# Token records in seven-word list entries, and filter rows of 2048 bytes

## The chip, the cores and the metric

The kernel runs on one core of a Trainium2 chip. Its engines are named as the profile names them: PE multiplies matrices (PEld is its weight load), DVE does elementwise work, ACT applies functions with a scale and a bias per row, POOL issues the indirect DMAs (gathers and scatters by lists of indices), SP issues all other DMAs. On chip there are SBUF, where every tile has 128 partitions, and PSUM, which PE writes.

The metric is the device time of one execution in microseconds (us). Before the change the median of six runs is 1482.05 us, with 1470.3 and 1488.45 as the ends.

## The reference, cut to what matters

The input is 16,384 tokens (16 x 1024) of 512 float32 values.

```python
xn = _layernorm(x)
# attention part
D = _fractal_dimension(xn)                       # one number, from the first 1024 values
x1 = ifft(fft(xn) * _wave_filter(D, 512)).real
lat = x1 @ W_el + b_el                           # 24 latents per token
bits = (sigmoid(lat) > 0.5)
s = x1 + _golay_correct(bits) @ W_le + b_le
# mixture of experts, 8 experts, the best 2 for each token
probs = softmax(xn @ router_w.T)
topk_vals, topk_idx = top_k(probs, 2)
topk_w = topk_vals / (topk_vals.sum(-1) + 1e-06)
combined = xn @ expert_weights[topk_idx]         # two products of 512 x 512 per token
g = _silu(((combined + topk_vals) * topk_w).sum())
out = x + s * g
```

`_golay_correct` takes 12 parity sums over the 24 bits and, if one to three of them are set, flips bits among the first 12.

## The kernel before

**Pass 1** goes through the tokens in order, in 128 tiles of 128 tokens, four tiles to a block. The filter is a circulant real operator, so it is worked out as matmuls in a basis in which a row's sum half, difference half and remaining half stay apart. For tile `g`:

- DVE adds the two halves of the row (`total`, L446); ACT turns the row's sum into a mean (`level`, L459) and takes the squares' sum (`spread`, L465); from it comes the token's scale (`scale`, L483 to L494).
- DVE folds the row (`fold`, L504 to L509), PE transposes it (`transpose`, L516) and ACT copies it out (L518).
- PE multiplies (`filt`): the sum part with `cs` (L532, 128 filter columns and 32 columns for latents and router logits), the difference part with `cd` (L533, the same widths), the rest with `cm` (L535). ACT scales the result into the block's buffer `yb` (L538), and every four tiles SP stores it into `yd` in DRAM (`store`, L545), a row of 576 words to a token: 128 columns of the sum, 32 + 32 latent columns, 128 of the difference, 256 of the rest.
- The latents and logits (`take_ex`, L561) go to `code` every 8 tiles: bits by comparison (L571), transposed through PE and ACT, parity sums by PE (L590), `correct` on DVE (L597 to L607). ACT copies the 12 bits that never change into the token's record (L588), `correct` writes the other 12 into it.
- They also go to `route` in eight rounds of 16 tiles: some 45 DVE operations and a few matmuls choose the two experts, the weights and the place of each token in one of 28 lists, one for each pair of experts. A record has 32 words a token: two weights, the bias (word 9), mean and scale (10, 11), the token's number (12), bits as bf16 (from word 13). At the end of a round 16 scatters on POOL (`scatter`, L787; one for each tile of 128 tokens) write words 10 to 12 of each record into `lists`, and `put_records` (L624) writes the whole records into the 32 columns `Q:XQ` of `yd`, four DMAs on SP a round.

101 tiles are filled by tokens of one pair of experts alone ("whole" tiles). Their entries are read by `whole_ops`, in two parts of 30 and 71 tiles: one gather `tt` (L907), taken apart by word on DVE (L918, L921), transposed on PE (L928), kept (L931 to L935). The other tiles fetch their entries one by one.

**Pass 2** takes tiles in the order of the lists: 28 whole tiles (the lead), 61 "item" tiles (leftovers of a pair, one expert at a time, results stored to `ed`), 5 whole tiles, and 27 "rest" tiles (which gather two stored item results) among 68 whole ones. For each tile POOL gathers the entry (`entry`, `rentry`), the token's `x` row (`xg`) and its filter row (`yg`, L1072 through `gather`; 8 buffers), and scatters the finished row (`put`, L1387). DVE normalises (L1237), ACT splits into halves (L1253), SP's transposing DMA turns them (L1258), ACT joins them (L1262), PE multiplies (L1295, 16 matmuls to a whole tile). ACT scales the first product with the weight from the record in `yg` (`scaled`, L1342), DVE adds the second with the other weight, and ACT applies silu with the bias (`added`, L1350, L1353). For the filter part DVE copies the bits three times (`triple`, L1310), PE turns them (`turn_code`, L1316) and multiplies them with `wle3`, three bf16 terms of `W_le` (`mend`, L1328). `spread_out` adds that to the row in two steps (L1333, L1334) and undoes the halves (L1336 to L1339); `combine` forms the result (L1381, L1382). "Item" tiles do none of these filter steps.

The order on every engine is that in which the code issues its instructions. Pass 1 runs a fixed list of steps per tile, with one scatter, one step of `code` and four of `route` among them. Pass 2 has due times per tile (`triple` three tiles ahead, `turn_code` two, `mend` one), and 3 scatters of the last round per tile until they are gone. `cs`, `cd` and `cm` are scaled and laid out once, in a setup that ends ahead of the first tile; `wle3` is filled from `setup_code`, two steps a tile. `clear` fills the four record buffers with zeros and a constant 1 for the `b_le` row.

## Time and profile before

| | |
|---|---|
| time of the profiled execution | 1480.49 us |
| its span, first to last instruction | 1478.7 us |
| mean granted clock of PE | 0.940 |
| PE busy | 1292.4 us (87%) |
| DVE busy | 913.2 us (62%) |
| ACT busy | 848.5 us (57%) |
| POOL busy | 768.7 us (52%) |
| L1295, the experts' products | 2104 matmuls, 605 ns each, 952.6 us |
| L535, L532, L533, the filter's products | 159.3, 66.6 and 61.1 us |
| L787, scatters | 128, 1031 ns each, 132.0 us |
| L1072 into `yg` | 101, 1118 ns each, 112.9 us |
| `yd<-yb` | 32 DMAs of 1152 KB |
| `yd<-rec` | 32 DMAs of 64 KB |
| packets under 512 bytes | 199543 of 265017 |

A profile is one execution. Busy is the time in which an engine has an instruction at work; the time ahead of an instruction in which its engine has nothing to do is put down to the one that released it, or to "issue" where the profile shows nothing that was waited for, or to "remote" where the releaser is not found among the recorded ones. The windows view gives the busy time of every engine in a stretch of time. Pass 1 ends at about 395 us. A group's count can lie a little under the true one, since some records are missing.

### The profile page before, as it was taken

The page shows a single profiled execution, that of the slowest core. Times are in us where ns is not written, and L with a number is a line of the kernel's source. Part 1 is how long each engine was busy: PE and PEld are TensorE (multiplying, and loading weights), DVE is VectorE, ACT ScalarE, POOL GpSimd, SP SyncE. Part 2 cuts the span into 40 slices and gives each one's busy share as a digit, 9 for nine tenths or more (in the row PEclk, how much of TensorE's full clock was granted, in tenths as well). Part 3 has the DMA queues.
Part 4 walks back from the last instruction along what each step waited for, and adds up shares of the span by engine and source line. Part 5 has one row for each costly group of instructions (what it writes and reads, how often), then busy time and mean ns, then how long its engine had stood idle before and what let it go on. Part 6 is the DMA issues. An engine that isn't in the chain of part 4 may idle for free.

```text
span 1478.7 us, 17021 instructions
## 1 busy us (share of the span) xinstructions
PE 1292.4 (87%) x4128; PEld 689.2 (47%) x4128; DVE 913.2 (62%) x2837; ACT 848.5 (57%) x1439; POOL 768.7 (52%) x743
## 2 busy tenths in 40 slices
PE   6977866977969699992989989998999999999996
PEld 5856755765624244440334434443444444444442
DVE  7866855865557368960111112787778777787885
ACT  7966855765434245551667676555555555555553
POOL 0044134224365755566656521677777776776741
PEclk9988878988989899996899999999999999999999
DMA  7996545743634476473879995788888888887861
GB/s 243 396 281 190 190 150 161 236 166 110 199 97 103 108 184 142 116 175 96 191 181 220 206 234 149 200 209 206 210 202 223 208 211 212 214 220 192 216 180 50
DMA packets 265017, 276.45 MB, mean 187 GB/s; under 512 B 199543, under 2 KB 200439, under 8 KB 260826
## 3 DMA queue, kind: packets, MB, share of 16 engines
q1 hardware_dynamic: 217114, 139.62, 37.0%
q0 software_dynamic: 47264, 135.54, 31.7%
q8 instruction: 37, 0.61, 0.2%
q14 instruction: 58, 0.48, 0.1%
q10 hardware_dynamic: 544, 0.21, 0.1%
HBM read 144.81 MB, written 89.59 MB: 159 GB/s over the span
## 4 chain that ended last, share of the span: by engine, by line
PE 62%; issue 10%; ACT 8%; another core or an unknown queue 7%; DVE 7%; DMA 2%; POOL 1%; ACTq 1%; SPq 0%; POOLq 0%; DVEq 0%
PE pe L1295 44%; PE py L535 7%; PE pt L516 3%; PE py L532 2%; ACT no L465 2%; PE py L533 2%; DVE acc L1350 1%; ACT yb L538 1%; DMA plt<-pl 1%; ACT pmt L518 1%; ACT xt L1262 1%; ACTq L1342 1%; PE pg L1328 1%; POOL out L1387 1%
## 5 line engine op out<-in xcount | busy, mean ns | idle before, releaser
L1295 PE MATMUL pe<-w_sb,xt 128*128 x2104 | 952.6, 605 | 54.7 <-ACT xt L1262 34.0
L1295 PEld LDWEIGHTS pe<-w_sb,xt 128*128 128x128 f32 x2104 | 404.1, 194 | 520.6 <-issue 465.2
L787 POOL DMA_INDIRECT lists<-rec,dst x128 | 132.0, 1031 | 284.7 <-ACT pmt L518 146.3
L1353 ACT ACTIVATE acc<-acc,yg 128x512 f32<-128x512 f32 x129 | 92.6, 719 | 252.6 <-DVE acc L1350 178.0
L1262 ACT COPY xt<-plt 128x1024 uint16<-128x1024 uint16 x156 | 209.0, 1340 | 22.3 <-DMA plt<-pl 21.2
L1350 DVE SCALAR_TENSOR_TENSOR acc<-pe,yg,acc 128x512 f32<-128x512 f32 (+1 forms) x102 | 75.7, 743 | 177.2 <-PE pe L1295 87.5
L1253 ACT COPY pl<-xn 128x1024 uint16<-128x1024 uint16 x156 | 162.1, 1039 | 0.0
L1237 DVE TENSOR_SCALAR xn<-xg,mean,entry 128x512 f32<-128x512 f32 x61 | 36.3, 595 | 200.8 <-ACT pl L1253 169.2
L1072 POOL DMA_INDIRECT yg<-yd,toks x101 | 112.9, 1118 | 90.4 <-ACT acc L1353 37.9
L535 PE MATMUL py<-cm,pmt 128*128 128x288 f32 x512 | 159.3, 437 | 0.0
L538 ACT ACTIVATE yb<-py,rec 128x640 f32<-128x640 f32 x128 | 102.2, 798 | 93.2 <-remote 42.2
L1387 POOL DMA_INDIRECT out<-xg,toks x100 | 108.9, 1089 | 70.9 <-DVE xg L1382 44.6
L1342 ACT ACTIVATE acc<-pe,yg 128x512 f32<-128x512 f32 x101 | 68.6, 680 | 132.4 <-PE pc L1316 32.7
L532 PE MATMUL py<-cs,pmt 128*128 128x160 f32 x256 | 66.6, 345 | 74.1 <-ACT pmt L518 47.6
L1072 POOL DMA_INDIRECT xg<-in_x,toks x100 | 106.7, 1067 | 46.4 <-issue 29.1
L535 PEld LDWEIGHTS py<-cm,pmt 128*128 128x128 f32 x512 | 99.7, 209 | 16.3
L465 ACT ACTIVATE no<-xt,sum 128x512 bf16<-128x512 f32 x128 | 91.8, 717 | 0.9 <-DVE pp L446 0.9
L1072 POOL DMA_INDIRECT part<-ed,adr_r x54 | 60.6, 1122 | 60.3 <-DMA ed<-res 44.2
L1382 DVE TENSOR_TENSOR xg<-mix,xg 128x512 f32<-128x512 f32 (+1 forms) x128 | 88.0, 687 | 4.4
L1072 POOL DMA_INDIRECT entry<-lists,adr_i x61 | 62.6, 1026 | 53.9 <-DVE mean L1236 28.9
L1381 DVE TENSOR_TENSOR mix<-mix,acc 128x512 f32<-128x512 f32 x129 | 87.7, 680 | 0.2 <-ACT acc L1353 0.2
L518 ACT COPY pmt<-pt 128x512 f32<-128x512 f32 x128 | 73.9, 578 | 18.5 <-remote 16.5
(282 smaller groups left out, 1627.8 us busy)
## 6 DMA issues: line engine op xcount, KB each, us to landing
yd<-yb SPq DMA_DIRECT2D x32, 1152.0 KB
xt<-in_x SPq DMA_DIRECT2D x32, 1024.0 KB
ed<-res SPq DMA_DIRECT2D x61, 256.0 KB
w_sb<-in_expert_w SPq DMA_DIRECT2D x8, 1024.0 KB
plt<-pl SPq DMA_TRANSPOSE x156
lists<-rec,dst POOLq DMA_INDIRECT x128
yd<-rec SPq DMA_DIRECT2D x32, 64.0 KB
yg<-yd,toks POOLq DMA_INDIRECT x101
```

What stands on the lines that cost most here:

```text
L465: nc.scalar.activation(no, xts[g // TPT][:, g % TPT, :], AF.Square, bias=k.sum[:, j : j + 1], scale=-float(E), accum_out=k.sq2[:, j : j + 1],)
L532: nc.tensor.matmul(py[:, 0, 0:XQ], pmt[:, 0, :], cs, start=True, stop=False)
L535: nc.tensor.matmul(py[:, 1, 0 : X + H], pmt[:, 2 + c, :], cm[:, c, :], start=(c == 0), stop=(c == 1))
L538: nc.scalar.activation(y_room(g), py[:, :, 0:WY], AF.Copy, scale=k.rec[:, j, 11:12])
L787: dma = nc.gpsimd.indirect_dma_start(out=lists, out_offset=bass.IndirectOffsetOnAxis(ap=st.dst[:, j : j + 1], axis=0), in_=st.rec.bitcast( ...
L1072: nc.gpsimd.indirect_dma_start(out=dst, out_offset=None, in_=src, in_offset=bass.IndirectOffsetOnAxis(ap=idx, axis=0), bounds_check=limit - 1,
L1253: nc.scalar.copy(k.pl.rearrange("p (h e) -> p h e", h=2), k.xn.bitcast(U16).rearrange("p (e h) -> p h e", h=2),)
L1262: nc.scalar.copy(k.xt.bitcast(U16).rearrange("p c (t h) -> p h c t", h=2), k.plt.rearrange("p (h c) t -> p h c t", h=2),)
L1295: nc.tensor.matmul(pe.unsqueeze(1), k.xt[:, c, :], w_sb[:, bass.ds(e, 1), c, :], start=(c == 0), stop=(c == KC - 1),)
L1350: nc.vector.scalar_tensor_tensor(k.acc[:, c], src[:, c], k.rec[:, 1:2], k.acc[:, c], ALU.mult, ALU.add)
L1353: nc.scalar.activation(k.acc[:, c], k.acc[:, c], AF.Silu, bias=k.rec[:, 9:10])
L1387: dma = nc.gpsimd.indirect_dma_start(out=of, out_offset=bass.IndirectOffsetOnAxis(ap=k.tok, axis=0), in_=k.x, in_offset=None, bounds_check ...
```

## The change

A list entry now has seven words and holds the whole record: two weights, bias, mean, scale, token and the 24 corrected bits as one whole number. Entries have 28 bytes rather than 12. The 32 record columns leave `yd`, whose rows become 512 words (2048 bytes) rather than 576 (2304).

- `put_records` and `clear` are gone, and ACT's copy of 12 bits (L588). `correct` writes the corrected bits in place, multiplies all 24 with powers of two and sums them into the word `BITS`: two more DVE operations, 16 times.
- The scatter sends words 0 to 6.
- `filt` writes the sum's and the difference's results by turns of 32 columns into PSUM (`by_turns`), with the latents and logits in the first 64 columns. `cs` has its latent columns in front. The stored 512 columns come behind the latents. `wle3` is filled in the same order: six copies rather than three.
- `whole_ops` takes seven words apart, with seven transposes rather than three and four DVE operations in `kept` rather than three.
- Weights, bias and bits come from the entry, not from the `yg` record.
- `triple` is a bitwise and of the tile's bits word with the powers of two (128 x 32 int32) and a comparison (128 x 96, to bf16) rather than one copy. For the entries past 24, whose power is 0, the comparison gives the constant 1 that the `b_le` row needs.
- `spread_out` adds the whole PSUM row in one operation (128 x 512) rather than in two of half the size; its last four operations stay, two of them reading and writing by turns of 32.

```diff
@@ -20,9 +20,8 @@
-META = 32
-ENTRY = slice(10, 13)
-BITS = 26
+W0, W1, BIAS, MEAN, SCALE, TOKEN, BITS, META = range(8)
+ENTRY = META
...
@@ -101,8 +99,8 @@
-    lists = dram.tile([NPAIR * N, 3], I32, name="lists")
-    yd = dram.tile([N, ROW], F32, name="yd")
+    lists = dram.tile([NPAIR * N, ENTRY], I32, name="lists")
+    yd = dram.tile([N, E], F32, name="yd")
...
@@ -249,10 +249,6 @@
-    def clear(r):
-        nc.vector.memset(r, 0.0)
-        nc.vector.memset(bits_of(r)[:, :, L : L + 1], 1.0)
-
...
@@ -375,10 +369,19 @@
+
+        def kept(k):
+            r = slice(32 * k, 32 * k + 32)
+            v.tensor_copy(
+                by_turns(wle3[r, 0:H]), term[r, 0:H].rearrange("p (a q c) -> p a q c", a=2, c=C)
+            )
+            v.tensor_copy(wle3[r, H:E], term[r, H:E])
+
...
+            lambda: v.tensor_copy(bit_i, bit_r),
@@ -391,15 +394,13 @@
-            lambda: v.tensor_copy(wle3[0:32, :], term[0:32, :]),
+            lambda: kept(0),
...
-                lambda k=k: v.tensor_copy(
-                    wle3[32 * k : 32 * k + 32, :], term[32 * k : 32 * k + 32, :]
-                ),
+                lambda k=k: kept(k),
...
@@ -517,6 +515,9 @@
+    def by_turns(a):
+        return a.rearrange("p (q a c) -> p a q c", a=2, c=C)
+
     def y_room(g: int):
@@ -529,14 +530,18 @@
-        nc.tensor.matmul(py[:, 0, 0:XQ], pmt[:, 0, :], cs, start=True, stop=False)
-        nc.tensor.matmul(py[:, 0, XQ:WY], pmt[:, 1, :], cd, start=False, stop=True)
+        both = by_turns(py[:, 0, 0:WY])
+        for a, w in enumerate((cs, cd)):
+            nc.tensor.matmul(
+                both[:, a], pmt[:, a, :], w.rearrange("p (q c) -> p q c", c=C),
+                start=(a == 0), stop=(a == 1),
+            )
         for c in range(2):
...
         nc.scalar.activation(
-            y_room(g), py[:, :, 0:WY], AF.Copy, scale=k.rec[:, j, 11:12]
+            y_room(g), py[:, :, 0:WY], AF.Copy, scale=k.rec[:, j, SCALE : SCALE + 1]
         )
@@ -544,7 +549,7 @@
             out=yd[b * BLK : (b + 1) * BLK, :].rearrange("(p j) n -> p j n", p=P),
-            in_=ybs[b].rearrange("p j h n -> p j (h n)")[:, :, 0:ROW],
+            in_=ybs[b].rearrange("p j h n -> p j (h n)")[:, :, 2 * X : 2 * X + E],
         )
@@ -558,7 +563,7 @@
         y = ybs[b][:, first:past]
-        nc.vector.tensor_add(to, y[:, :, 0, Q:XQ], y[:, :, 0, XQ : XQ + X])
+        nc.vector.tensor_add(to, y[:, :, 0, 0:X], y[:, :, 0, X : 2 * X])
         nc.vector.tensor_add(to, to, y[:, :, 1, H : H + X])
@@ -585,7 +590,6 @@
-            nc.scalar.copy(bits_of(k.rec)[:, :, 12:L], k.bits[:, :, 12:L])
@@ -605,8 +609,15 @@
             nc.vector.tensor_tensor(
-                bits_of(k.rec)[:, :, 0:12], k.bits[:, :, 0:12], fix, ALU.not_equal
-            )
+                k.bits[:, :, 0:12], k.bits[:, :, 0:12], fix, ALU.not_equal
+            )
+            worth = small.tile([P, GT, L], F32, name="worth", bufs=1)
+            nc.vector.tensor_mul(
+                worth, k.bits, bit_r[:, 0:L].unsqueeze(1).to_broadcast([P, GT, L])
+            )
+            with nc.allow_low_precision("whole numbers below 2 to the 24th"):
+                nc.vector.tensor_reduce(k.rec.bitcast(I32)[:, :, BITS], worth, AX.X, ALU.add)
+            k.packed = True
@@ -618,14 +629,6 @@
-    def put_records(t, n, r=None):
-        r = r or recs[(t // (2 * GT)) % 4]
-        for a in range(t, t + n, TPT):
-            nc.sync.dma_start(
-                out=yd[a * P : (a + TPT) * P, Q:XQ].rearrange("(p j) m -> p j m", p=P),
-                in_=r[:, a % (2 * GT) : a % (2 * GT) + TPT, :],
-            )
-
...
@@ -783,11 +786,11 @@
         def scatter(j):
-
+            assert groups[(t0 + j) // GT].packed
             dma = nc.gpsimd.indirect_dma_start(
...
                 out_offset=bass.IndirectOffsetOnAxis(ap=st.dst[:, j : j + 1], axis=0),
-                in_=st.rec.bitcast(I32)[:, j, ENTRY],
+                in_=st.rec.bitcast(I32)[:, j, 0:ENTRY],
                 in_offset=None,
@@ -815,17 +818,17 @@
-            lambda: v.tensor_add(st.rec[:, :, 9], st.ch[:, 0, :], st.ch[:, 1, :]),
+            lambda: v.tensor_add(st.rec[:, :, BIAS], st.ch[:, 0, :], st.ch[:, 1, :]),
...
-            lambda: v.tensor_add(st.rec[:, :, 0], st.wt[:, 1, :], st.lo),
-            lambda: v.tensor_sub(st.rec[:, :, 1], st.wt[:, 0, :], st.lo),
+            lambda: v.tensor_add(st.rec[:, :, W0], st.wt[:, 1, :], st.lo),
+            lambda: v.tensor_sub(st.rec[:, :, W1], st.wt[:, 0, :], st.lo),
...
-        return ops + ranks + [lambda: put_records(t0, S)]
+        return ops + ranks
...
@@ -903,7 +907,7 @@
             nc.vector.tensor_copy(woff[part], k.pi)
-            k.tt = mid.tile([P, P, 3], I32, name="tt")
+            k.tt = mid.tile([P, P, ENTRY], I32, name="tt")
             nc.gpsimd.indirect_dma_start(
@@ -914,25 +918,29 @@
-            k.tf = mid.tile([P, 3, P], F32, name="ttf")
+            k.tf = mid.tile([P, ENTRY, P], F32, name="ttf")
...
-                k.tf[0:n, 0:2, :], k.tt.bitcast(F32)[0:n, :, 0:2].rearrange("t c o -> t o c")
-            )
-            nc.vector.tensor_copy(k.tf[0:n, 2, :], k.tt[0:n, :, 2])
+                k.tf[0:n, 0:TOKEN, :],
+                k.tt.bitcast(F32)[0:n, :, 0:TOKEN].rearrange("t c o -> t o c"),
+            )
+            nc.vector.tensor_copy(
+                k.tf[0:n, TOKEN:, :], k.tt[0:n, :, TOKEN:].rearrange("t c o -> t o c")
+            )
...
-            k.pt = ps_g.tile([P, 512], F32, name="pg")[:, 0 : 3 * n].rearrange(
-                "p (o t) -> p o t", o=3
-            )
-            for o in range(3):
+            k.pt = ps_g.tile([P, 512], F32, name="pg")[:, 0 : ENTRY * n].rearrange(
+                "p (o t) -> p o t", o=ENTRY
+            )
+            for o in range(ENTRY):
...
-            nc.vector.tensor_copy(toks[part], k.pt[:, 2, :])
+            nc.vector.tensor_copy(toks[part], k.pt[:, TOKEN, :])
+            nc.vector.tensor_copy(masks[part], k.pt[:, BITS, :])
+            nc.vector.tensor_copy(stats[part], k.pt[:, 0:TOKEN, :])
...
-                stats[part][:, 0, :], k.pt[:, 0, :], -0.25, None, ALU.mult
-            )
-            nc.vector.tensor_copy(stats[part][:, 1, :], k.pt[:, 1, :])
+                stats[part][:, MEAN, :], stats[part][:, MEAN, :], -0.25, None, ALU.mult
+            )
...
@@ -1188,19 +1193,24 @@
             k.tok = toks[part][:, t : t + 1]
-            k.mean, k.scale = (stats[part][:, i, t : t + 1] for i in range(2))
+            k.bits = masks[part][:, t : t + 1]
+            k.w0, k.w1, k.bias, k.mean, k.scale = (
+                stats[part][:, i, t : t + 1] for i in range(TOKEN)
+            )
             return
         if k.kind == "item":
-            entry = w2.tile([P, 3], I32, name="entry", bufs=16)
+            entry = w2.tile([P, ENTRY], I32, name="entry", bufs=16)
             assert ("item", k.n // GI * GI) in ready
...
             assert ("rest", 0, k.n >= half) in ready
-            entry = w2.tile([P, 3], I32, name="rentry", bufs=NREST)
+            entry = w2.tile([P, ENTRY], I32, name="rentry", bufs=NREST)
             adr = adr_r[:, 0, k.n : k.n + 1]
         gather(entry, lists, adr, NPAIR * N)
-        k.tok = entry[:, 2:3]
-        k.low, k.scale = (entry.bitcast(F32)[:, i : i + 1] for i in range(2))
+        k.tok, k.bits = (entry[:, i : i + 1] for i in (TOKEN, BITS))
+        k.w0, k.w1, k.bias, k.low, k.scale = (
+            entry.bitcast(F32)[:, i : i + 1] for i in range(TOKEN)
+        )
@@ -1212,11 +1222,8 @@
             return
-        row = w2.tile([P, ROW], F32, name="yg", bufs=8)
-        gather(row, yd, k.tok, N)
-        k.rec = row[:, Q:XQ]
-        k.sd = row[:, 0 : 2 * (XQ + X)].rearrange("p (a n) -> p a n", a=2)[:, :, 0:Q]
-        k.m = row[:, WY:ROW]
+        k.row = w2.tile([P, E], F32, name="yg", bufs=8)
+        gather(k.row, yd, k.tok, N)
@@ -1306,8 +1313,14 @@
-        bits = k.rec.bitcast(BF16)[:, BITS : BITS + 32]
-        nc.vector.tensor_copy(k.b3, bits.unsqueeze(1).to_broadcast([P, 3, 32]))
+        some = w2.tile([P, 32], I32, name="some", bufs=2)
+        nc.vector.tensor_tensor(some, k.bits.to_broadcast([P, 32]), bit_i, ALU.bitwise_and)
+        nc.vector.tensor_tensor(
+            k.b3,
+            some.unsqueeze(1).to_broadcast([P, 3, 32]),
+            bit_i.unsqueeze(1).to_broadcast([P, 3, 32]),
+            ALU.is_equal,
+        )
@@ -1330,16 +1343,17 @@
             return
-        nc.vector.tensor_add(k.sd, k.pw[:, 0:H].rearrange("p (a n) -> p a n", a=2), k.sd)
-        nc.vector.tensor_add(k.m, k.pw[:, H:E], k.m)
+        nc.vector.tensor_add(k.row, k.pw, k.row)
         k.mix = w2.tile([P, E], F32, name="mix", bufs=3)
-        nc.vector.tensor_add(k.mix[:, 0:Q], k.sd[:, 0, :], k.sd[:, 1, :])
-        nc.vector.tensor_sub(k.mix[:, Q:H], k.sd[:, 0, :], k.sd[:, 1, :])
-        nc.vector.tensor_sub(k.mix[:, H:E], k.mix[:, 0:H], k.m)
-        nc.vector.tensor_add(k.mix[:, 0:H], k.mix[:, 0:H], k.m)
+        sd, m = by_turns(k.row[:, 0:H]), k.row[:, H:E]
+        mix = k.mix[:, 0:H].rearrange("p (a q c) -> p a q c", a=2, c=C)
+        nc.vector.tensor_add(mix[:, 0], sd[:, 0], sd[:, 1])
+        nc.vector.tensor_sub(mix[:, 1], sd[:, 0], sd[:, 1])
+        nc.vector.tensor_sub(k.mix[:, H:E], k.mix[:, 0:H], m)
+        nc.vector.tensor_add(k.mix[:, 0:H], k.mix[:, 0:H], m)
     def scaled(out, src, k):
-        nc.scalar.activation(out, src, AF.Copy, scale=k.rec[:, 0:1])
+        nc.scalar.activation(out, src, AF.Copy, scale=k.w0)
@@ -1348,9 +1362,9 @@
             nc.vector.scalar_tensor_tensor(
-                k.acc[:, c], src[:, c], k.rec[:, 1:2], k.acc[:, c], ALU.mult, ALU.add
-            )
-            nc.scalar.activation(k.acc[:, c], k.acc[:, c], AF.Silu, bias=k.rec[:, 9:10])
+                k.acc[:, c], src[:, c], k.w1, k.acc[:, c], ALU.mult, ALU.add
+            )
+            nc.scalar.activation(k.acc[:, c], k.acc[:, c], AF.Silu, bias=k.bias)
@@ -1598,7 +1612,12 @@
-        [base, *(ends[1:] - ends[:-1]).T, np.asarray(L0_attn_b_el)]
+        [
+            base,
+            *(ends[1:] - ends[:-1]).T,
+            np.asarray(L0_attn_b_el),
+            [2.0**i if i < len(golay_t) else 0.0 for i in range(32)],
+        ]
```

The index shifts from `11:12` to `SCALE` and the like, in `level`, `scale`, `fold` and `filt`, are left out where nothing else changes.

## The prediction, made before the changed kernel ran

> **What bounds the kernel now.** I read the chain of waits first, then the windows by stage, then the timeline where an engine stands idle, last the groups by form for prices.
>
> ```profile
> PE 62%; issue 10%; ACT 8%; another core or an unknown queue 7%; DVE 7%; DMA 2%; POOL 1%; ACTq 1%; SPq 0%; POOLq 0%; DVEq 0%
> ```
>
> PE sets most of the end. DMA and SP's queue, which the change relieves most visibly, hold 2% and 0%. The windows (PE, PEld, DVE, ACT, POOL busy with instructions in brackets, PE's clock, DMA share, GB/s) show two kinds of time in pass 1, then the lead (530 to 650) and the rest tiles (905 to 1430):
>
> ```profile
> 261.00:283.00 22.00, 21.89 (x131) 18.27 (x130) 19.98 (x91) 19.65 (x49) 0.00 (x0) 0.95 0.63 219
> 283.00:312.00 29.00, 18.43 (x93) 13.83 (x92) 13.47 (x66) 14.34 (x37) 17.42 (x17) 0.82 0.52 157
> 530.00:650.00 120.00, 120.00 (x305) 54.41 (x304) 103.09 (x246) 64.21 (x83) 66.15 (x61) 1.00 0.56 139
> 905.00:1430.00 525.00, 508.00 (x1290) 226.51 (x1289) 403.92 (x998) 288.94 (x421) 367.27 (x331) 0.99 0.80 207
> ```
>
> While POOL is quiet, pass 1 is bound by PE, with DVE and ACT close behind. While POOL issues a round's 16 scatters (second line), all three fall idle. The timeline inside such a burst (start, duration, idle time before with its releaser) shows how:
>
> ```profile
> 245.92 0.58 ACT L518 COPY pmt<-pt 128x512 f32<-128x512 f32 x1 [2.41 <-remote]
> 249.85 0.38 PE L516 MATMUL pt<-ident,mm 128*128 128x128 f32 x2
> 252.23 0.97 POOL L787 DMA_INDIRECT lists<-rec,dst  x1 [0.30 <-issue]
> 255.23 0.79 ACT L538 ACTIVATE yb<-py,rec 128x640 f32<-128x640 f32 x1 [8.72 <-remote]
> 255.97 0.35 DVE L504 SCALAR_TENSOR_TENSOR sd<-pp,rec 128x128 f32<-128x128 f32 x1 [9.00 <-remote]
> ```
>
> ACT and DVE wait about 9 us for nothing that the records show, though PE had gone on. Tiles come every 2.0 us in the quiet (L538 starts at 126.26, 128.22, 130.23); by the second window seven bursts of 29 us lose 29 - 18.4 = 11, some 12 with the slower clock: about 85 us. The 128 scatters stay, so I let this loss stay. In the lead PE has no gap at all; with the rest tiles it lacks 17 of 525 us.
>
> ```profile
> 402.59 1.00 POOL L1072 DMA_INDIRECT yg<-yd,toks  x1 [5.06 <-DVE xn L1237]
> 406.41 0.69 ACT L1342 ACTIVATE acc<-pe,yg 128x512 f32<-128x512 f32 x1 [9.59 <-DMA yg<-yd,toks]
> ...
> 457.31 2.58 SPq L624 DMA_DIRECT2D yd<-rec  x4
> 458.99 0.62 DVE L783 TENSOR_REDUCE dst<-pl 128x16 int32<-128x448 f32 x1
> 462.23 1.01 POOL L1072 DMA_INDIRECT yg<-yd,toks  x1 [12.86 <-DVE mix L1338]
> 465.21 0.99 POOL L787 DMA_INDIRECT lists<-rec,dst  x1 [0.30 <-issue]
> ```
>
> At the passes' seam ACT waits for the first filter row, since its weight lies in it; and POOL stands 12.86 us ahead of a row until the last round's records have been written to `yd` (the releaser printed had long been done).
>
> **The change, part by part.** Prices come from the groups by form (busy, mean ns):
>
> ```profile
> L1381 DVE TENSOR_TENSOR mix<-mix,acc 128x512 f32<-128x512 f32 x127 | 86.8, 684 | 0.0
> L1333 DVE TENSOR_TENSOR yg<-pg,yg 128x256 f32<-128x256 f32 x100 | 41.3, 413 | 3.6 <-PE pg L1328 3.6
> L1310 DVE COPY b<-yg 128x96 bf16<-128x96 bf16 x128 | 24.2, 192 | 3.5 <-PE pc L1316 3.5
> L571 DVE TENSOR_TENSOR bits<-ex,negb 128x192 bf16<-128x192 f32 x16 | 5.7, 353 | 0.0
> L677 DVE TENSOR_REDUCE athot<-eq 128x16 f32<-128x128 f32 x16 | 4.5, 282 | 0.3
> L588 ACT COPY rec<-bits 128x96 bf16<-128x96 bf16 x16 | 4.5, 279 | 0.0
> L754 PE MATMUL pg<-q,ones_b 128*128 128x336 bf16 x8 | 2.4, 306 | 0.0
> L761 PE MATMUL pg<-oh,ones_b 128*128 128x336 bf16 x8 | 2.4, 305 | 0.0
> ```
>
> *Gone, in pass 1.* 16 ACT copies, 16 x 0.279 = 4.5 us of an engine with 2.35 of 22 us free in the quiet: a gain of 0 to 4.5, I take 1, since PE is fuller. The zeroing of four record buffers, 4 x (485 + 72 ns) = 2.2 us on DVE: 0 to 2.2, I take 0, because it lies ahead of the flow or beside loads. `put_records`: 32 DMAs are 16,384 packets of 128 bytes at 13 ns, 212 us of queue time or 13.3 us on each of 16 engines; the rows shrink by 11% besides. The x loads keep DVE waiting 0.2 us in all pass 1, so 0 in the flow. At its end the last stores land sooner: 0 to 2, I take 1.
>
> *The seam.* Without the records' write the first L1342 needs no filter row. PE's own idle time after it is 2.6 us, ACT's 9.59: gain 0 to 9.6, I take 3. POOL needs the last round's destinations before the scatter now at 465.21: they are there at 458.99 + 0.62, plus 0.70 for the longer `correct`, so the scatter can begin near 460.3, 4.9 us sooner; all of the 12.86 at the most. PE works without a gap from 443 to 474, so little reaches the end: I take 2. Sum of gains: 1 + 0 + 1 + 3 + 2 = 7.
>
> *Added, `correct`.* A 128 x 192 product is like L571, 353 ns. The sum over 24 is a reduction of 192; L677 reduces 128 in 282; with about 1 ns for each of the 64 further elements I estimate 345: 16 x 0.70 = 11.2 us of DVE. Half of the 16 lie in bursts, where DVE idles; a tile group takes 8 x 2.0 = 16 us, in which DVE has 16 x 2.02/22 = 1.5 us free. Loss 0 to 11.2, I take 1.
>
> *Added, pass 2.* Starts follow one another by 0.11 us behind L1310, by 0.33 and 0.34 for the two adds, by 0.71 for a 128 x 512 operation. The two new bit operations depend on each other: some 0.22 + 0.17, so +0.28; the merged add +0.04: 0.32 us a tile, 41 us of DVE over 128 tiles. The cover is PE: in the lead DVE has 17 of 120 us free and needs 4 more for 12 tiles, with the rest tiles 121 of 525 and needs 95 x 0.32 = 30. Where PE waits for the triple itself (11.8 us in all behind L1310) the delay shows. I take 2; the bound is 41.
>
> *Added, `whole_ops`.* Four more transposes in each of two parts (some 0.25 us), one more DVE operation and larger ones, a larger gather: 0 to 3, I take 1. It is off the lead's way until the 31st tile.
>
> *Added, scatters.* POOL's price goes by instruction: entries of 12 bytes 1026 to 1031 ns, xg of 2048 bytes 1067, yg of 2304 1118. 28 bytes lie next to 12, so 0; upper bound 128 x 0.087 = 11 us of POOL, which pass 1 would feel in its bursts. Gathered rows are shorter (1118 to 1067 at best), with POOL's idle time covering both.
>
> *Moved: columns by turns of 32 in PSUM.* L761 writes PSUM in turns of 28 words or more, L754 without gaps: 305 and 306 ns, and 258 against 261 for 224 columns. So 0. [...]
>
> Losses: 1 + 2 + 1 = 4. Net 7 - 4 = 3 us: 1480.5 - 3 = 1477.5 for an execution like the profiled one, which lies 1.6 below the median of the runs: 1479.
>
> **Rivals.** Half a per cent, 7.4 us, is what a measurement here can tell from no change: faster is below 1474.6, slower above 1489.5.
>
> *A, the forecast:* 1479, own range 1467 to 1490: the seam's two gains at their bounds would take 9.6 - 3 and 4.9 - 2, and `correct` and half the rest tiles' DVE work would add 10. Chance 0.45.
>
> *B, the bursts shorten.* In each round `put_records`' 2048 packets run at the same time as the scatters' small ones. If that pressure is part of what delays PE's results, a quarter of 85 us goes, 21: 1458. For: bursts are the largest loss, and small packets are their mark. Against: in the burst shown the long wait falls where no SP transfer ran. Chance 0.22.
>
> *C, slower: DVE becomes the pace.* In the quiet stretches DVE is busy 19.98 of 22 us; in the rest tiles it must mix a row before its buffer is free. If half of the added DVE work shows (16 x 0.70/2 = 5.6 in pass 1, half of 30 = 15 with the rest tiles, 3 of the lead's 5.4), 24 us replace my 4: 1499. It decides once the windows show DVE above 98% of PE's time; by busy time it stands at 103 + 4 of 120, which is against it; in-order waits speak for it. Chance 0.27.
>
> *D, strided PSUM writes cost.* L532 and L533 have two records a tile of 345 and 323 ns; were their pace of about 0.55 us a tile doubled over the 80 tiles in the quiet, +44: 1523. Chance 0.06.
>
> That the change doesn't do what it says I exclude: in the order in which the changed program's instructions stand, L624's writes and L588 are gone, and POOL and PE have as many rows as before.
>
> **How the numbers follow.** Of A 0.17 lies faster, 0.235 the same, 0.045 slower; of B 0.21 and 0.01; of C 0.04 the same and 0.23 slower; D slower. Faster 0.38, same 0.28, slower 0.34 (rounded). The range runs from 1453 (B with some room) to 1502 (C with some), leaving out D and the tails.
>
> **What would show it.** No L624, L588; POOL's last round begins near 460 (the seam); tiles still 2.0 us apart in the quiet and L532 at 345 ns (D false); scatters near 1031 ns (12 against 28 bytes); burst windows still lose 11 us (B false) or less; DVE busy about 913 + 11 + 41 - 2 = 963 us, with PE still full between 530 and 650 (C false). A burst that grows longer, or PE gaps behind the bit operations in the rest tiles, would make the forecast wrong.

## The result, and the profile after

The changed kernel was slower: 1507.92 us median (20 runs, 1499.65 to 1516.76) against 1483.92 for before (46 runs, 1470.3 to 1498.1), a ratio of 1.0176 with a 95% interval of 1.0155 to 1.0196. The profiled execution took 1505.48 us, its span is 1503.2. Which chip these are from the results don't say; four further sets, on chips that they number 12, 4, 7 and 15, gave 0.9959 (0.9881 to 1.0036), 0.9897 (0.9839 to 0.9954), 0.9851 (0.9780 to 0.9922) and 0.9979 (0.9933 to 1.0024). On chips 4 and 7 before itself takes 1297 us, not 1465 or more. That is the main finding, and the experiments turn on it. (A ratio leaves disturbed runs out, so two medians need not agree with it.)

The chain of waits of the profile after, which had PE 62%, issue 10%, ACT 8%, DVE 7% before:

```profile
PE 61%; issue 11%; DVE 10%; another core or an unknown queue 7%; ACT 5%; DMA 3%; POOL 1%; ACTq 0%; POOLq 0%; SPq 0%; DVEq 0%
```

The windows after (us, then busy time of PE, PEld, DVE, ACT, POOL with instructions in brackets, PE's clock, DMA share, GB/s): a burst and a quiet stretch of pass 1, the lead, and the rest stage from the first to the last joined tile behind the items.

```profile
281.00:310.00 29.00, 18.97 (x82) 13.05 (x81) 13.95 (x65) 13.29 (x32) 16.83 (x17) 0.71 0.36 119
310.00:332.00 22.00, 22.00 (x139) 18.43 (x139) 20.97 (x93) 19.68 (x47) 0.00 (x0) 1.00 0.65 227
530.00:650.00 120.00, 116.74 (x302) 52.98 (x301) 101.83 (x234) 59.79 (x80) 61.44 (x57) 1.00 0.58 140
914.30:1476.40 562.10, 535.19 (x1341) 238.14 (x1340) 447.14 (x1039) 300.62 (x441) 371.04 (x335) 0.98 0.72 191
```

The same rest stage before the change, by the same two events:

```profile
906.80:1451.60 544.80, 527.80 (x1340) 235.49 (x1339) 421.10 (x1041) 301.63 (x441) 371.40 (x335) 0.99 0.79 202
```

Bursts still leave PE idle for a third of their time, and the quiet stretch is as full as before. Counting by events (start of the last scaling in pass 1, then of the first, 25th, 35th, 84th and last joining on ACT, L1262 before and L1269 after; the first six tiles are turned on PE and not joined), pass 1 took 391.8 us rather than 393.8, the seam up to the first joined tile 67.5 rather than 59.7, the lead 193.5 rather than 189.8, the next stretch, in which the items start, 72.1 rather than 68.3, the items 189.4 rather than 195.3 and the rest stage 562.1 rather than 544.8. The tail is equal. So of the 24.5 us 17.3 lie in the rest stage and 7.8 at the seam; what the lead and the next stretch lose beside them (3.7 and 3.8) the items and pass 1 give back. These are one profile each.

The groups by form after:

```profile
L540 PE MATMUL py<-cm,pmt 128*128 128x288 f32 x512 | 160.5, 440 | 0.0
L790 POOL DMA_INDIRECT lists<-rec,dst x128 | 131.1, 1024 | 295.7 <-ACT yb L543 145.2 <-DVE sd L505 76.5 <-issue 35.4
...
L1346 DVE TENSOR_TENSOR yg<-pg,yg 128x512 f32<-128x512 f32 x100 | 68.3, 683 | 3.5 <-PE pg L1341 3.5
L535 PE MATMUL py<-cs,pmt 128*128 128x160 f32 x256 | 65.4, 340 | 70.9 <-issue 38.5 <-ACT pmt L516 32.4
...
L535 PE MATMUL py<-cd,pmt 128*128 128x160 f32 x256 | 59.9, 318 | 0.0
...
L1318 DVE TENSOR_TENSOR b<-some,bit_i 128x96 bf16<-128x96 int32 x128 | 33.1, 258 | 7.5 <-PE pc L1329 3.1
...
L1317 DVE TENSOR_TENSOR some<-masks,bit_i 128x32 int32<-128x32 int32 x101 | 18.4, 182 | 0.0
...
L615 DVE TENSOR_TENSOR worth<-bits,row_sb 128x192 f32<-128x192 bf16 x16 | 5.7, 358 | 0.6
L619 DVE TENSOR_REDUCE rec<-worth 128x8 int32<-128x192 f32 x16 | 5.7, 355 | 0.6
```

The prices that the prediction set hold. The matmuls that write PSUM by turns of 32 columns are no longer than before (340 and 318 ns, where 345 and 323 were), scatters of 28 bytes take 1024 ns (1031), `correct`'s additions 358 and 355 ns (353 and 345 foreseen; the 1 ns an element in it is an estimate that two of its rows give, (684 - 353) / 320 = 1.03). Of the two bit operations the second starts 0.22 us behind the first, and the next operation 0.18 behind the second (starts at 1002.57, 1002.79 and 1002.97 in the timeline after; 0.22 and 0.17 foreseen). DVE's busy time rose by 45 us, 50 foreseen. The sum was not wrong by the price of an instruction.

A stretch of the rest stage, from the timeline after (start, duration, idle time before with its releaser; lines of other engines left out), shows results that come late:

```profile
1225.93 3.60 PE L1302 MATMUL pe<-w_sb,xt 128*128 x8
...
1228.28 0.69 ACT L1356 ACTIVATE acc<-pe,stats 128x512 f32<-128x512 f32 x1 [3.48 <-remote]
...
1230.77 1.03 POOL L1401 DMA_INDIRECT out<-xg,toks  x1 [0.30 <-issue]
...
1232.11 1.02 POOL L1080 DMA_INDIRECT xg<-in_x,rentry  x1 [0.31 <-issue]
...
1233.98 0.75 DVE L1364 SCALAR_TENSOR_TENSOR acc<-pe,stats,acc 128x512 f32<-128x512 f32 x1 [5.72 <-remote]
...
1238.67 1.17 POOL L1080 DMA_INDIRECT part<-ed,adr_r  x1 [5.54 <-ACT acc L1356]
```

The eight matmuls of a product end at 1229.5, and DVE takes the result up at 1233.98, right after POOL, which had gone from DMA to DMA with gaps of 0.3 us, fell idle at 1233.1. DVE then ran back to back for 28.5 us (1233.98 to 1262.48), tile after tile, to catch up.

### The profile page after: what moved, and what is told of

The parts are those of the page before. It is cut to its first block, busy times and chain, and to the rows that moved or that the text cites. A ratio compares the mean times of both kernels' runs of the same rounds, so it can differ in the third digit from the quotient of the medians.

```text
span 1503.2 us, 17125 instructions
## 1 busy us (share of the span) xinstructions
PE 1304.6 (87%) x4136; PEld 693.4 (46%) x4136; DVE 958.4 (64%) x2867; ACT 845.5 (56%) x1423; POOL 767.8 (51%) x743
## 4 chain that ended last, share of the span: by engine, by line
PE 61%; issue 11%; DVE 10%; another core or an unknown queue 7%; ACT 5%; DMA 3%; POOL 1%; ACTq 0%; POOLq 0%; SPq 0%; DVEq 0%
PE pe L1302 42%; PE py L540 8%; PE py L535 5%; PE pt L514 4%; DMA plt<-pl 2%; DVE acc L1364 2%; ACT xt L1269 1%; ACT no L463 1%; DVE mix L1395 1%; DVE yg L1346 1%; PE pg L1341 1%; DVE mix L1352 1%; ACT pl L1260 1%; DVE xn L1244 1%
## 5 line engine op out<-in xcount | busy, mean ns | idle before, releaser
L1302 PE MATMUL pe<-w_sb,xt 128*128 x2104 | 962.6, 611 | 60.7 <-issue 30.1
L1302 PEld LDWEIGHTS pe<-w_sb,xt 128*128 128x128 f32 x2104 | 408.7, 196 | 532.2 <-issue 484.8
L790 POOL DMA_INDIRECT lists<-rec,dst x128 | 131.1, 1024 | 295.7 <-ACT yb L543 145.2
L1269 ACT COPY xt<-plt 128x1024 uint16<-128x1024 uint16 x156 | 208.9, 1339 | 32.3 <-DMA plt<-pl 30.1
L1367 ACT ACTIVATE acc<-acc,stats 128x512 f32<-128x512 f32 (+1 forms) x102 | 73.1, 718 | 244.8 <-DVE acc L1364 196.5
L1364 DVE SCALAR_TENSOR_TENSOR acc<-pe,stats,acc 128x512 f32<-128x512 f32 (+1 forms) x102 | 75.6, 742 | 162.5 <-remote 70.9
L1080 POOL DMA_INDIRECT yg<-yd,toks x101 | 109.0, 1080 | 53.0 <-issue 25.5
L1356 ACT ACTIVATE acc<-pe,stats 128x512 f32<-128x512 f32 x101 | 68.4, 677 | 115.3 <-remote 56.8
```

Of the source, the lines that this page charges most:

```text
L790: dma = nc.gpsimd.indirect_dma_start(out=lists, out_offset=bass.IndirectOffsetOnAxis(ap=st.dst[:, j : j + 1], axis=0), in_=st.rec.bitcast( ...
L1080: nc.gpsimd.indirect_dma_start(out=dst, out_offset=None, in_=src, in_offset=bass.IndirectOffsetOnAxis(ap=idx, axis=0), bounds_check=limit - 1,
L1269: nc.scalar.copy(k.xt.bitcast(U16).rearrange("p c (t h) -> p h c t", h=2), k.plt.rearrange("p (h c) t -> p h c t", h=2),)
L1302: nc.tensor.matmul(pe.unsqueeze(1), k.xt[:, c, :], w_sb[:, bass.ds(e, 1), c, :], start=(c == 0), stop=(c == KC - 1),)
L1364: nc.vector.scalar_tensor_tensor(k.acc[:, c], src[:, c], k.w1, k.acc[:, c], ALU.mult, ALU.add)
```

## The experiments

Four theories were tried. P: DVE became the pace beside the rest tiles. S: the loss is at the seam. B: while POOL issues indirect DMAs back to back, the news that PE is done reaches ACT and DVE late, and the change shifts where such runs fall. W, a sharper B: the change took a wait from POOL in pass 2, so its runs grew.

**The same kernel again (e1_again, chip 12).** No edit.

> The changed kernel once more, for a second profile. Theory P (DVE is the pace beside the rest tiles): the rest stage, from the 84th to the last joined tile, again takes 17 us longer than before, and DVE's catching-up period is near 4.9 us a tile. Theory S (the loss sits in the seam between the passes and in POOL's bursts there and is carried on): the rest stage's share changes from profile to profile by 10 us or more. 1508 either way.

1470.29 us against 1464.8 for before, ratio 0.9959: no loss that can be told from none, where 1508 was expected. The rest stage of its profile took 551.4 us, 10.7 less than on the first chip. Single runs of either kernel spread over 30 us here (1445 to 1478).

**Bits from a constant (e1_const, chip 12).** It leaves the tokens' bits out.

```diff
-        some = w2.tile([P, 32], I32, name="some", bufs=2)
-        nc.vector.tensor_tensor(some, k.bits.to_broadcast([P, 32]), bit_i, ALU.bitwise_and)
-        nc.vector.tensor_tensor(
-            k.b3,
-            some.unsqueeze(1).to_broadcast([P, 3, 32]),
-            bit_i.unsqueeze(1).to_broadcast([P, 3, 32]),
-            ALU.is_equal,
-        )
+        nc.vector.tensor_copy(k.b3, ident_b[:, 0:32].unsqueeze(1).to_broadcast([P, 3, 32]))
```

> The changed kernel with one copy of a constant of the same shape in place of the two bit operations (the bits of the tokens are left out), so that DVE has 0.28 us a tile less and the chain from the bits to PE is as short as before. P: most of the 17 us of the rest stage and a few of the lead come back, 1485 to 1492. S: within 4 us of 1508.

1470.71 us, ratio 1.0070 (1.0011 to 1.0128), beside 1470.29 and 0.9959 with the bit operations: nothing came back. Its rest stage, by the windows, in an execution of 1481.13 us:

```profile
901.60:1452.10 550.50, 529.09 (x1340) 237.02 (x1339) 426.37 (x943) 301.68 (x440) 368.73 (x335) 0.98 0.74 195
```

DVE has some 21 us less to do than in the changed kernel (447 to 448 in its three profiles where results come late), and the stage is no shorter.

**The add in two again (e1_twoadd, chip 12).**

```diff
-        nc.vector.tensor_add(k.row, k.pw, k.row)
+        nc.vector.tensor_add(k.row[:, 0:H], k.pw[:, 0:H], k.row[:, 0:H])
+        nc.vector.tensor_add(k.row[:, H:E], k.pw[:, H:E], k.row[:, H:E])
```

> The changed kernel with the PSUM row added in two operations of 128x256, as before, in place of one of 128x512. P: 0.04 us a tile less on DVE, 1504 to 1508. If the merged add is what costs (the longer hold of the row and of PSUM), 1490 to 1500. S: 1508.

1487.36 us (4 runs, ratio 1.0155, 1.0080 to 1.0230), rest stage 567.8. A miss for every theory: an edit of some 0.04 us a tile on DVE (0.71 us from start to start in one operation, 0.33 and 0.34 in two) came out about 17 us, 1.2%, slower than the changed kernel beside it, and where the first result was. Why, no run shows.

**Before with two more operations (e1_bplus, chip 12).**

```diff
+        some = w2.tile([P, 32], I32, name="some", bufs=1)
+        nc.vector.tensor_tensor(
+            some, ident.bitcast(I32)[:, 0:1].to_broadcast([P, 32]),
+            ident.bitcast(I32)[:, 0:32], ALU.bitwise_and,
+        )
+        same = w2.tile([P, 3, 32], BF16, name="same", bufs=1)
+        nc.vector.tensor_tensor(
+            same,
+            some.unsqueeze(1).to_broadcast([P, 3, 32]),
+            some.unsqueeze(1).to_broadcast([P, 3, 32]),
+            ALU.is_equal,
+        )
         nc.vector.tensor_copy(k.b3, bits.unsqueeze(1).to_broadcast([P, 3, 32]))
```

> The kernel before with two operations added in front of its copy of the bits, of the shapes of the two bit operations (128x32 and, dependent on it, 128x96; their results are not used): 0.39 us a tile more on DVE. P: 20 to 28 us longer than before, 1504 to 1512, nearly all of it beside the rest tiles. S: within 4 us of 1484.

1463.55 us, ratio 1.0009 (0.9951 to 1.0067). Its rest stage:

```profile
885.40:1426.10 540.70, 527.18 (x1341) 233.83 (x1340) 454.35 (x1233) 299.42 (x440) 372.55 (x335) 1.00 0.78 204
```

More DVE work (454 us) than the changed kernel has, and a stage as short as before's 544.8 on the first chip (before itself was not profiled on chip 12). With e1_const, P falls from both sides on this chip: DVE's added work is covered, as the prediction had it.

This run also serves as a kernel before to set beside e1_again, since its pass 1 is before's. Their spans are alike, 1452.9 and 1452.1 us, but not their stages: the changed kernel took 64.7 us rather than 57.1 at the seam and 551.4 rather than 540.7 in the rest stage, as on the first chip, and 372.9 rather than 390.3 for pass 1. So the chip without a loss has the same two losses, and a shorter pass 1 hides them. Why pass 1 was so much shorter there, no run shows.

**Four kernels on a chip of the other kind (chip 4).** e2_again is the changed kernel. e2_yg7 has seven buffers for `yg` (`bufs=8` to `bufs=7`). The other two let a scatter wait for its tile:

```diff
         def scatter(j):
+            d = small.tile([P, 1], I32, name="dj", bufs=20)
+            nc.vector.tensor_copy(d, st.dst[:, j : j + 1])
...
-                out_offset=bass.IndirectOffsetOnAxis(ap=st.dst[:, j : j + 1], axis=0),
+                out_offset=bass.IndirectOffsetOnAxis(ap=d, axis=0),
```

(e2_bgate does so in the kernel before, with eight such buffers.)

> The changed kernel once more, beside before, in five rounds, to fix how far it is slower. Two earlier sets of runs gave ratios of 1.0176 and 0.9959. Theory P (DVE is the pace beside the rest tiles): rest stage 12 to 20 us longer than before's in any set, the ratio above 1.008. Theory B (bursts of POOL's indirect DMAs hold up the news that PE is done; the change only shifts where bursts fall): the ratio is scattered from set to set, and the loss sits where bursts became longer.

> The changed kernel with seven buffers for the filter rows rather than eight, so that POOL waits for a later mix on DVE ahead of each gather, about where it waited for ACT's silu before. B: POOL's runs of 20 and more DMAs beside the rest tiles are cut, the rest stage loses 5 to 15 us against the changed kernel's. P: unchanged or slower, within 3 us of the changed kernel or above.

> The changed kernel with a copy of the scatter's 128 places on DVE ahead of each scatter, at the point in the tile's order where the scatter stands (one a tile in pass 1), so that a round's 16 scatters go one a tile and not back to back. B: pass 1's bursts lose far less than 12 us each: pass 1 ends 30 to 80 us sooner than the changed kernel's 373 to 392. Rival (the loss is a fixed price of each scatter, some 0.7 us): pass 1 ends within 10 us of it.

> The kernel before with the same copy ahead of each scatter. B: 30 to 80 us faster than before; rival: within 10 us.

Before took 1297.19 us, the changed kernel 1285.96 (ratio 0.9897), e2_yg7 1285.67 (0.9896), e2_gate 1301.25 (1.0027), e2_bgate 1298.61 (0.9991). Before and the changed kernel are 168 and 184 us faster than on chip 12, and PE is busy for 1214.8 of the 1235 us from 25 to 1260 in e2_again, so pacing had little to win. e2_gate took 15.3 us more than e2_again; the 128 copies are 18.8 us of DVE, at the 147 ns of e4_gate's profile. By the letter the two paced kernels landed where the rival said; since B is about results that come late, and here they do not, the set decides nothing on it.

**Before and after on chip 7.** e3_before is the kernel before, for its profile; e3_again, e3_yg7 and e3_gate as above.

> The kernel before, for a profile of it on the chip that runs the next three. Theory B says: if PE's results arrive late while POOL issues back to back, as in the first profiles (1484 and 1465 us), pass 1 ends near 390 and the rest stage takes 540 or more; if they do not (1297 us in the last set), pass 1 ends near 306 and the rest stage takes 517.

> The changed kernel beside before. B: where PE's results come late, 0 to 2% slower than before, with the rest stage 10 to 17 us longer; where they do not, 0.5 to 1.3% faster, pass 1 shorter and the rest stage the same 517 us.

> Seven buffers for the filter rows. Where PE's results come late, B: the rest stage 5 to 15 us shorter than the changed kernel's, since POOL pauses more often. If the length of POOL's runs does not matter, within 3 us. Where they do not come late, no difference, as in the last set.

> One scatter a tile. Where PE's results come late, B: pass 1 ends 30 to 80 us sooner than the changed kernel's; rival (a fixed price of each scatter): within 10 us. Where they do not come late, pass 1 ends 8 us later, as in the last set, for the copies.

1288.27 us (one run), 1281.44 (0.9851), 1281.81 (0.9843) and 1301.79 (1.0063), with before at 1297.0 over 13 runs. Windows of e3_again, one over the whole of a burst of 16 scatters (149.4 to 170.9) and one over the rest stage:

```profile
149.00:172.00 23.00, 23.00 (x142) 19.30 (x141) 21.87 (x97) 22.94 (x59) 16.93 (x16) 1.00 0.79 254
...
735.90:1253.30 517.40, 517.40 (x1341) 234.47 (x1340) 449.32 (x1039) 299.56 (x440) 380.75 (x335) 1.00 0.81 207
```

and the rest stage of e3_before:

```profile
742.30:1259.30 517.00, 517.00 (x1340) 234.19 (x1339) 421.36 (x1041) 302.18 (x440) 374.69 (x335) 1.00 0.83 213
```

Here 16 scatters go back to back, at 1067 ns each in this profile (1024 on the first chip), and PE has no gap beside them (23.00 of 23 us). The rest stage is full with PE in both kernels (517.40 of 517.4 us and 517.00 of 517.0), at a granted clock of 1.00. By the same events as above the changed kernel took 299.3 us for pass 1 (before 304.8), 44.0 for the seam (49.3), 179.4 for the lead (173.9), 33.4 where the items start (33.4), 179.8 for the items (180.9) and 517.4 for the rest (517.0). In one profile each the whole is 6.4 us less; the medians are 15.6 apart, and where the remaining 9 us lie is not shown.

**The same on a chip where results come late (chip 15).** e4_again, e4_yg7 and e4_gate as above. e4_actrow makes ACT read the filter row, as it did before; it leaves the experts' bias out, with a filter column in its place.

```diff
-            nc.scalar.activation(k.acc[:, c], k.acc[:, c], AF.Silu, bias=k.bias)
+            nc.scalar.activation(k.acc[:, c], k.acc[:, c], AF.Silu, bias=k.row[:, 0:1])
```

> The changed kernel beside before. Where PE's results come late (before at 1465 or more): 0 to 2% slower, rest stage 10 to 17 us longer than before's. Where they do not (before near 1297): 1.0 to 1.5% faster.

> The changed kernel with silu's bias read from the filter row (the bias of the experts is left out, a filter column stands in its place), so that ACT again releases the row's buffer and POOL waits for it as before. Theory W (the wait taken from POOL lets its runs of DMAs grow, and PE's results wait for their end): where results come late, 8 to 20 us faster than the changed kernel, with the rest stage back at before's. Rival: within 4 us of the changed kernel, so the loss has another cause. Where they do not come late: within 4 us.

> Seven buffers for the filter rows. W: where results come late, 5 to 15 us faster than the changed kernel; rival: within 4 us. Where they do not come late: within 4 us, as in two sets.

> One scatter a tile. Where results come late, theory B: pass 1 ends 30 to 80 us sooner than the changed kernel's; rival (a fixed price of each scatter): within 10 us. Where they do not: 1.5% slower than the changed kernel, as in two sets.

| chip 15, before 1465.33 us | median | ratio to before | rest stage | seam |
|---|---|---|---|---|
| e4_again | 1468.27 | 0.9979 (0.9933 to 1.0024) | 550.1 | 67.0 |
| e4_actrow | 1460.21 | 0.9974 (0.9927 to 1.0021) | 541.6 | 67.3 |
| e4_yg7 | 1451.87 | 0.9940 (0.9897 to 0.9982) | 536.9 | 51.8 |
| e4_gate | 1382.84 | 0.9444 (0.9380 to 0.9508) | 545.0 | 52.0 |

e4_again lost nothing that can be told from none, a miss. Theory B is shown for pass 1 by e4_gate. Two bursts' stretches and all of pass 1, of e4_again first:

```profile
120.00:150.00 30.00, 18.32 (x102) 14.99 (x101) 15.79 (x67) 16.65 (x40) 15.96 (x16) 0.89 0.42 143
170.00:200.00 30.00, 17.89 (x97) 14.40 (x95) 15.05 (x66) 15.20 (x37) 15.87 (x16) 0.79 0.43 143
0.00:382.40 382.40, 305.97 (x1711) 250.11 (x1711) 276.32 (x1227) 271.46 (x650) 109.86 (x129) 0.91 0.58 202
```

then of e4_gate:

```profile
120.00:150.00 30.00, 29.31 (x177) 23.92 (x176) 28.93 (x138) 27.67 (x68) 13.89 (x14) 1.00 0.73 226
170.00:200.00 30.00, 29.33 (x176) 23.70 (x175) 28.96 (x140) 27.67 (x67) 13.84 (x15) 1.00 0.75 239
0.00:307.40 307.40, 288.20 (x1711) 235.55 (x1711) 278.39 (x1324) 269.61 (x650) 108.99 (x129) 0.98 0.75 251
```

The same scatters, one to a tile with a short wait between, and PE is busy 29.3 of 30 us at a granted clock of 1.00; pass 1 takes 75 us less. The loss was neither a price of the scatter (1033 ns in e4_again, 1038 in e4_gate) nor of its bytes, but of scatters without a pause. The records of PE's semaphore agree: stretches of over 5 us without an update, though matmuls ended in them, add up to 66 us of pass 1 in e4_again and to 11 in e4_gate.

The seam column goes the same way. Take POOL's DMAs with less than 0.6 us between them as one run. In the six profiles of a changed kernel with eight `yg` buffers and unpaced scatters, where results come late, POOL makes one run of 31 DMAs at the seam, and the seam takes 63.6 to 67.5 us (e4_actrow is one of them). In the two of before (the first chip and e1_bplus) it makes runs of 20 and 11, and the seam takes 59.7 and 57.1. e4_yg7 cuts the run to 15 and 18 DMAs and takes 51.8; e4_gate cuts it to 16 with short groups behind it and takes 52.0. These two are one profile each, but lie over 11 us below all six. Where the run breaks, a filter row's gather waits for a buffer. Shown are the ninth row in before, which waits 5.99 us; the ninth after, which does not, and the eleventh, which does; and the eighth in e4_yg7:

```profile
434.51 1.01 POOL L1072 DMA_INDIRECT yg<-yd,toks  x1 [5.99 <-ACT pl L1253]
...
426.52 1.01 POOL L1080 DMA_INDIRECT yg<-yd,toks  x1 [0.30 <-DVE mix L1352]
...
450.66 1.01 POOL L1080 DMA_INDIRECT yg<-yd,toks  x1 [9.68 <-DVE mix L1353]
...
413.76 1.01 POOL L1080 DMA_INDIRECT yg<-yd,toks  x1 [2.64 <-DVE mix L1353]
```

For W, the waits of POOL in the rest stage (line, releaser, us in total, times, longest). The profile after on the first chip:

```profile
POOL part L1080 <- ACT acc L1356: 37.5, 13, 6.9
...
POOL yg L1080 <- DVE mix L1353: 22.5, 11, 5.4
```

and e4_actrow:

```profile
POOL yg L1080 <- ACT ct L1333: 23.8, 16, 3.2
...
POOL yg L1080 <- ACT acc L1367: 21.5, 10, 3.1
```

The kernel before had the second pattern: 26.4 us behind ACT's ct and 22.3 behind its silu, each wait 3.6 us or less, and no wait of `part` for ACT. In the changed kernel POOL runs past the filter row's gather and then stands, up to 6.9 us at a time, before `part`. e4_actrow put the short waits back, and the rest stage took 541.6 us, as in before (544.8) and e1_bplus (540.7), where the changed kernel's three profiles on such chips have 562.1, 551.4 and 550.1. e4_yg7 has a wait of another kind at the same place and 536.9. As whole times e4_actrow and e4_again can't be told apart by their ratios, and e4_yg7's interval overlaps e4_again's.

The traces speak against W in the rest stage. POOL's runs did not grow there: its 335 DMAs make runs of 11.6 on average and 31 at the longest in before, of 11.2 and 25 in the changed kernel on the first chip. e4_gate has the changed kernel's code in this stage and its waits (20.0 us of `part` behind ACT, 5.0 the longest), and its stage took 545.0, as long as before's. Nor does the length go by how late results are: the stretches without an update of PE's semaphore add up to 201 us of the rest stage in e4_again and to 259 in e4_actrow, whose stage is 8.5 us shorter. So W is not shown, and what made the rest stage longer stays open.

**Both together, and before paced (chip 4 again).** e5_bgate is e2_bgate. e5_all is e2_gate with seven `yg` buffers and `entry` at `bufs=6` rather than 16.

> The kernel before with one scatter a tile. Where results come late: theory B, 4 to 7% faster than before, pass 1 ends near 310 as on the two other chips; if it is within 0.5% of e4_gate's ratio of 0.944, the change loses or wins nothing beside the bursts. Where they do not come late: the same as before, as in an earlier set.

> The changed kernel with one scatter a tile, seven buffers for filter rows and six rather than sixteen for the item tiles' entries, so that POOL's run of some 40 DMAs where the item tiles start is broken up too (that stretch takes 71 us where results come late, 33 where they do not). Theory B, where results come late: 10 to 40 us faster than 0.944 of before, the stretch below 60 us. Where they do not: 1 to 2% slower than the changed kernel, for the copies.

1301.08 us (1.0021) and 1299.03 (1.0011), before 1298.33. Results were not late on this chip, so both questions stay open: whether paced scatters serve the kernel before as well on a late chip, and what pacing the items' gathers is worth there.

## Why the prediction was wrong

- **The forecast of no change** was 1479, range 1453 to 1502; the result, 1507.92, lies above it. Rival C had the sign, with 1499, but not the cause: on chip 12 e1_bplus and e1_const show that DVE's added work costs nothing that can be measured, as the paragraph "Added, pass 2" said in its main term. The ratios of chips 12 and 15, 0.9959 and 0.9979, are what was forecast, but by luck: the changed kernel's seam is as long there (64.7 and 67.0 us) as on the first chip.
- **The step that failed** is "The seam", and with it the 2 us that "Added, pass 2" takes for all of pass 2. The prediction counts POOL's part in busy time and takes a wait that POOL loses for a gain of 0 or more. It put no price on the longer run of DMAs that follows, though it had read how results come late beside such a run in pass 1. At the seam the runs show a loss of 7.8 us where 5 were to be won, and a run of 31 DMAs in place of 20 and 11; split by e4_yg7, the seam is shorter than before's. The rest stage took 17.3 us more on the first chip. By chip 12 DVE's work is not the cause, and POOL's runs were not longer there; the cause stays open. That the release of the filter row's buffer moved from ACT's silu to DVE's mix was not costed either, under "Gathered rows are shorter, with POOL's idle time covering both". It is not shown to be the cause: e4_actrow moves it back, and at the seam it changes nothing (67.3 us, a run of 31).
- **The seam**, forecast as a gain of 3 + 2 us, was a loss of 7.8 on the first chip. The chain of waits after shows why, with DVE waiting twice for results that PE had ready; the timeline's lines of PE and DVE follow:

```profile
414.11 7.42 another core or an unknown queue
...
429.63 14.63 another core or an unknown queue
...
444.32 0.75 DVE acc L1364
...
414.49 0.60 PE L1253 MATMUL pt<-ident,xn 128*128 128x128 f32 x4
422.55 0.34 PE L1329 MATMUL pc<-ident_b,b 128*96 128x128 bf16 x1 [7.46 <-DVE b L1318]
...
435.64 0.60 PE L1253 MATMUL pt<-ident,xn 128*128 128x128 f32 x4
448.00 0.34 PE L1329 MATMUL pc<-ident_b,b 128*96 128x128 bf16 x1 [11.76 <-DVE b L1318]
...
444.32 0.75 DVE L1364 SCALAR_TENSOR_TENSOR acc<-pe,stats,acc 128x512 f32<-128x512 f32 x1 [14.69 <-remote]
```

PE stood idle from 415.1 and from 436.2, so what DVE waited for had ended; the updates of PE's semaphore that let DVE go are recorded at 421.53 and 444.26, and DVE started 0.03 and 0.06 us later. It was the news that was late, not DVE. POOL ran from 400.1 to 441.0 there, 31 DMAs without a pause; before, it had made two runs of 20 and 11. The sign that the prediction named, POOL's last round near 460 rather than 465.21, failed with it:

```profile
466.31 0.99 POOL L790 DMA_INDIRECT lists<-rec,dst  x1 [13.32 <-DVE mo L803]
```

(PE's work "without a gap from 443 to 474" had one gap before, 0.96 us at 445.24; nothing rests on it.) On chip 7, with results on time, the seam gained 5.3 us, close to the 5 of the sum.
- **Bursts.** "The 128 scatters stay, so I let this loss stay" held (pass 1 was 2.0 us shorter). Rival B's reason for bursts, `put_records`' small packets, falls: without them a burst's window loses as much (10.0 of 29 us, 10.6 before), and e4_gate removes the loss with all scatters' packets in place.
- **Right:** writing PSUM by turns of 32 columns cost nothing here: no run shows the doubling of rival D (340 and 318 ns after, 345 and 323 before; 316 and 300 against 319 and 302 on chip 7); 28-byte entries cost POOL at most 21 ns each (1024 ns against 1031; 1067 against 1046 on chip 7); the gains of pass 1 exist, 5.5 us on chip 7 against 1 + 1 - 1 foreseen; and without late results the kernel is faster by 1.0 to 1.5%, though more than the 3 us of the sum. In the lead chip 7 shows 5.5 us lost; 3 were foreseen for all of pass 2 and `whole_ops` together. The sign "PE still full between 530 and 650" held nearly (116.7 of 120 us on the first chip).
- **Open:** what made the rest stage longer, and why the first chip's loss is 24 us and those of chips 12 and 15 are near 0. On chip 12 the difference lies in pass 1. e1_twoadd, with 0.04 us a tile moved, lay 17 us above e1_again on the same chip; what decides it, no run shows.

## What to carry to other kernels

Ask of a wait that is removed what the engine does next, and whether that hurts another: at the seam POOL's waits were pauses in which the others got their results (63.6 to 67.5 us with one run of 31 DMAs, 51.8 and 52.0 with runs of 15 to 18). An idle time whose releaser is "remote" while the producer has long been done is a cost to be explained before a change is priced, and running the same program on a second chip tests it. Tie each indirect DMA to its tile, not all of them to a round: in the changed kernel a copy of 147 ns took 5.8% off the time where results came late, and cost 1.2 to 1.6% where they did not. In the kernel before it was not run where results come late.

## What the hardware showed

Whether PE's results arrive late beside POOL's runs differs from chip to chip: before took 1465 to 1484 us in three sets (chips 12, 15 and the first) and 1297 to 1298 in three others (chips 4 and 7), with the same program and input. PE's mean granted clock differs with it: 0.940 against 0.987 in the profiles of before. In the records of semaphore events the stretches of over 5 us without one from PE, though matmuls ended in them, add up to 559 us in before and 665 after on the first chip, and to 60 and 33 on chip 7. What in the chips makes the difference, no run here shows.
